# A four-layer graph network on one core: in the search for edges, TensorE's order within a turn and the grouping of three blocks are changed

## The chip, the cores and the metric

The kernel runs on one core of a Trainium2 chip. The metric is the device time of one execution in microseconds (us). Five engines work at once, each through its own instructions in order: TensorE (PE in the profile, its weight loads PEld), VectorE (DVE), ScalarE (ACT), GpSimd (POOL) and SyncE (SP). SP, ACT and POOL also issue DMA transfers; POOL alone issues the indirect ones, in which a list of row numbers chooses the rows.

## The reference, cut to what matters

There are 2708 nodes with 512 features each and one weighted adjacency matrix, which is mostly zero. Each layer is a sum over neighbours, added to its input and normalised along the features.

```
x = layernorm(x + d*(adj+I)*d @ x @ W0.T + b0)          # d: row sums to the power -1/2
x = layernorm(x + (inc @ x) / rowsum(inc))               # inc = adj + (adj>0)/sqrt(count of adj>0)
x = layernorm(x + sigmoid(ga * softmax-like(adj) @ (x@Wsa) + gb * (adj @ x @ Wg + bg)))
x = layernorm(x + relu(adj @ (x>0) @ sign(W3).T))
```

All four layers use the same nonzero pattern of `adj`. A zero entry adds nothing in any of them.

## The kernel before

The nodes are cut into 22 blocks of 128 rows, the last (21) of 20. `adj` is dense in memory and mostly zero, so the kernel first **searches**: for every block of output rows it finds the nodes that have an edge to it, lists them in tiles of 128, and fetches only those rows of the transposed matrix into `packed[b]`. The number of tiles of each block is fixed ahead (`ROOM`: 4, 4, 3 and 1 for blocks 18 to 21). Afterwards the four layers multiply the packed tiles with gathered feature rows.

The search goes in **turns**, `turn(at)`, one for each block in the order 1 to 21 and then 0 (`arrival`). Blocks are handled in **groups** (`GROUPS`): the lists of a group are made together, some turns after its last block. Within a turn all engines' instructions are kept in the order in which the code calls the steps (`in_order`), so the order of the calls is each engine's order. The steps are:

- `load_x`, `load` (SP): the features and the adjacency rows of the block two turns ahead, `arow`, in two halves of 128x1408 and 128x1300. There are four such buffers, so a load waits until the halves of two blocks before have been read.
- `sum_rows` (ACT, L840): row sums of the block's two halves. `degrees` (L848 to L683) makes `dinv` of them for two blocks at a time.
- `mark` (DVE L904, L911, L917; PE L925): a 0/1 mask of the nonzeros, and then 22 small products that count, for each node, the block's edges. They go to a PSUM tile `find`, one for each group out of a ring of two. The remaining steps of VectorE are mixed in between the two halves of the mask.
- `own_diagonals`, `count` (DVE L936 to L981): one turn after the group's last block, the counts become places in a list. `count_partitions` (PE L989) follows after the marks of that turn.
- `steps_of` (DVE L1000 to L1005, PE L1008), `look_up` (ACT L1017, DVE L1029 and L1034, PE L1041) and `keep_looked` (ACT L1051), two turns after it, and `list_nodes` (DVE L1059 to L1078), three turns after it, turn the places into row numbers, `row_at`. For the group (2, 3) all of this happens in the turn after its last block.
- `fetch` (POOL L1099): one indirect DMA of 128 rows for every listed tile. After every second one of the earlier groups a short memset (L1105) makes POOL rest; `RESTED` leaves out the last groups.
- `transpose_x` (PE L1118), `keep_transposed` (ACT L1125), `project0` (PE L1133, four fp32 products of 128x512, shown as eight records), `scale0` (ACT L1142, L1143), `fold` (DVE L1150, L1154) and `grow0` (PE L1161): the first layer's features times `W0`. `y_rows` in memory receives each block's product, and block 0, which is dense, is summed on the way.

Before the change, TensorE's turn `at` is: `steps_of`, marks of block `at`, `count_partitions`, transposes of block `at`, `look_up`, product of block `at-1`, `grow0` of `at-3`.

After the search the layers run over `sequence` = 0, 1, 21, 2, ..., 20. POOL gathers the rows (L626: `xg` from `y_rows` in the first layer, from `x1_rows`, shown as x_rows, in the second), PE multiplies (L1396 in both), DVE and ACT normalise (L1511, L688 to L704). While the first layer runs, the heads of the second are made for one group at a time, at fixed places of `sequence` (`between`): `count_positive` (DVE L1191, PE L1193) and then `head_steps` (DVE L1213 to L1232, ACT L1219, PE L1237, ACT L1245). In the first layer and later, a scheduler mixes the steps of neighbouring blocks. The first gather of a layer waits for all rows that the layer before has written.

Of the kernel before, what the change touches and what calls it, by code (L numbers as in the profile page):

```python
# [52 lines left out]
)  # L53

GROUPS = (
    (1,), (2, 3), (4, 5), (6, 7, 8), (9, 10, 11), (12, 13, 14), (15, 16, 17), (18, 19, 20), (21,),
)


# [448 lines left out]
def sparse_layers(ctx, tc, x, adj, adj_t, w0_t, b0, w_sa, a_sa, w_gcnb, b_gcnb, wa, ba, wb, bb, w3_t,  # L508
# [19 lines left out]
    def rows(b: int) -> int:  # L528
        return min(P, N - b * P)
# [5 lines left out]
    def tiles(b: int) -> int:  # L535
        return len(direct(b)) + ROOM[b]
# [50 lines left out]
    def narrow(b: int) -> int:  # L587
        return len(SPANS[SPLIT[b]])
# [82 lines left out]
    def newton_steps(dst, v, r0, r1, n: int):  # L671
        def square():
            if n == 1:
                nc.vector.scalar_tensor_tensor(r1, r0, v, r0, op0=ALU.mult, op1=ALU.mult)
            else:
                nc.vector.tensor_tensor(r1, r0, v, op=ALU.mult)
                nc.vector.tensor_tensor(r1, r1, r0, op=ALU.mult)

        return [
            lambda: nc.vector.reciprocal(r0, r0),  # L680
            square,
            lambda: nc.vector.tensor_scalar(r1, r1, -0.5, 1.5, op0=ALU.mult, op1=ALU.add),
            lambda: nc.vector.tensor_tensor(dst, r0, r1, op=ALU.mult),  # L683
        ]
# [34 lines left out]
    with tc.tile_pool(name="s_pre", bufs=1) as pre:  # L719
# [65 lines left out]
        turn_at, at = {}, 0  # L785
        for g in GROUPS:
            turn_at[g] = at
            for b in g:
                n, more = narrow(b), ROOM[b] - narrow(b)
# [54 lines left out]
        def degrees(bs):  # L844

            b, n, m = bs[0], len(bs), rows(bs[0])
            deg = small.tile([P, 2], F32, tag="deg", name=f"deg{b}")[:m, :n]
            nc.vector.scalar_tensor_tensor(  # L848
                deg, row_sums[:m, b : b + n, 0], 1.0, row_sums[:m, b : b + n, 1],
                op0=ALU.add, op1=ALU.add,  # L850
            )
            root_ = small.tile([P, 2, 2], F32, tag="root", name=f"root{b}")
            nc.scalar.activation(root_[:m, 0, :n], deg, AF.Sqrt)
            return newton_steps(
                dinv[:m, b : b + n], deg, root_[:m, 0, :n], root_[:m, 1, :n], n
            )

        def due_degrees(at: int):

            if at == NTURN or at == NTURN - 1:  # L860
                return (arrival[at - 1],)
            return tuple(arrival[at - 2 : at]) if 0 < at < NTURN and at % 2 == 0 else ()
# [67 lines left out]
        def own_diagonals(g):  # L930

            b0_, G, m = g[0], len(g), rows(g[0])
            if own_by_itself(b0_):
                own = search[g]["find"][:, b0_ * KINDS : (b0_ + G * (NB + 1)) * KINDS]
                own = own.rearrange("p (g q) -> p g q", g=G)
                nc.vector.scalar_tensor_tensor(  # L936
                    dia_own[:m, b0_ : b0_ + G], own[:m, :, KINDS - 1], 0.0,
                    dia[:m, b0_ : b0_ + G], op0=ALU.is_equal, op1=ALU.mult,
                )

                own = own[:m, :, : KINDS - 1]
                nc.vector.tensor_tensor(own, own, foreign[:m, b0_ : b0_ + G, :], op=ALU.add)
# [43 lines left out]
        def count_partitions(g):  # L986

            b0_, G = g[0], len(g)
            nc.tensor.matmul(  # L989
                search[g]["before"].rearrange("p (c g) -> p c g", g=G), tri,  # L990
                found[:, :, b0_ : b0_ + G], start=True, stop=True,
            )

        def steps_of(g):

            b0_, G = g[0], len(g)
            n = KINDS * G
            diff = search[g]["diff"]
            base = small.tile([P, 2, KINDS * GM], F32, tag="base", name=f"base{b0_}")
            nc.vector.tensor_copy(base[:, 0, :n], search[g]["before"])  # L1000
            nc.vector.tensor_scalar(
                base[:, 1, :n], base[:, 0, :n], WHOLE128, WHOLE128, op0=ALU.add, op1=ALU.subtract
            )
            nc.vector.tensor_copy(table[:, :n, NB], base[:, 1, :n])
            nc.vector.tensor_tensor(  # L1005
                table[:, :n, NB + 1], base[:, 0, :n], base[:, 1, :n], op=ALU.subtract
            )
            nc.tensor.matmul(  # L1008
                diff, step, table[:, :n].rearrange("p k c -> p (k c)"), start=True, stop=True
            )  # L1010
            search[g]["base"] = base
# [36 lines left out]
        def keep_looked(g):  # L1048
            T = sum(ROOM[b] for b in g)
            look = pre.tile([P, TS, NT], F32, tag="look", name=f"look{g[0]}", bufs=2)  # L1050
            nc.scalar.copy(look[:, :T], search[g]["looked"])  # L1051
            search[g]["look"] = look
# [37 lines left out]
                at += ROOM[b]  # L1090

        to_fetch = []
        RESTED = GROUPS[:-2]
        fetched = [0]
        rest = pre.tile([P, 384], F32, name="s_rest")

        def fetch(n: int):
            for b, t, row in to_fetch[:n]:
                nc.gpsimd.indirect_dma_start(  # L1099
                    out=packed[b][:, t + len(direct(b)), :], out_offset=None, in_=adj_t,  # L1100
                    in_offset=bass.IndirectOffsetOnAxis(ap=row, axis=0), element_offset=b * P,
                )
                fetched[0] += 1
                if group_of[b] in RESTED and fetched[0] % 2 == 0:
                    nc.gpsimd.memset(rest, 0.0)  # L1105
            del to_fetch[:n]
# [145 lines left out]
        def count_block0():  # L1252

            for h, ar in enumerate(arows.pop(0)):
                nc.vector.tensor_scalar(
                    ar, ar, 0.0, 0.0, op0=ALU.is_gt, op1=ALU.add, accum_out=counts0[:, h : h + 1]
                )
# [7 lines left out]
        def each(action, at: int):  # L1265
            if 0 <= at < NTURN:
                action(arrival[at])

        def turn(at: int):
            step_of = {at - last_at[g]: g for g in GROUPS[1:]}  # L1270

            def chain(action, since: int):
                if step_of.get(since, SOON) != SOON:
                    action(step_of[since])

            steps = degrees(due_degrees(at)) if due_degrees(at) else []
            chain(steps_of, 2)
            each(sum_rows, at)
            each(keep_transposed, at - 1)
            found_in = step_of.get(1)  # L1280

            if found_in:
                steps.insert(0, lambda: count(found_in))
                steps.insert(0, lambda: own_diagonals(found_in))
            if at < NTURN and arrival[at]:
                mark(arrival[at], steps)
            else:
                for step_ in steps:
                    step_()
            if found_in:  # L1290
                count_partitions(found_in)
                if found_in == SOON:
                    steps_of(SOON)
            each(load_x, at + 2)
            each(load, at + 2)
            each(transpose_x, at)
            chain(look_up, 2)
            chain(list_nodes, 3)
            if found_in == SOON:
                look_up(SOON)  # L1300
                keep_looked(SOON)
            if at == 0:
                for step_ in (
                    count, count_partitions, steps_of, look_up, keep_looked, list_nodes
                ):
                    step_(GROUPS[0])
            each(scale0, at - 2)
            each(project0, at - 1)
            chain(keep_looked, 2)
            each(fold, at - 3)  # L1310
            each(grow0, at - 3)
            if found_in == SOON:
                list_nodes(SOON)
            fetch(len(to_fetch))
            if at == NTURN:
                count_block0()

        with in_order():
            for at in range(NTURN + 4):
                turn(at)  # L1320
# [87 lines left out]
    with tc.tile_pool(name="s_l0", bufs=10, reuse_waits="tile") as lp:  # L1408
# [60 lines left out]
        def several(*actions):  # L1469
            def act():  # L1470
                for a in actions:
                    a()
            return act
# [2 lines left out]
        counts()  # L1476
        roots()
        several(*others)()
        for n, g in enumerate(GROUPS):
            steps_ = head_steps(g)  # L1480
            between.setdefault(2 + 2 * n, []).append(
                several(lambda g=g: count_positive(g, lp), steps_[0])
            )
            between.setdefault(3 + 2 * n, []).append(several(*steps_[1:]))
# [111 lines left out]
    with tc.tile_pool(name="s_l1", bufs=8, reuse_waits="tile") as lp:  # L1596
# [67 lines left out]
        for at, b in enumerate(sequence):  # L1664
            m = rows(b)
            if b:
# [23 lines left out]
                for i0, r0, w, a in narrow_views(b):  # L1690
                    n = a.shape[1]
# [322 lines left out]
    with tc.tile_pool(name="s_l3", bufs=11, reuse_waits="tile") as lp, \  # L2014
# [96 lines left out]
        for at, b in enumerate(order3):  # L2111
# [21 lines left out]
            for i0 in range(0, tiles(b), CH3):  # L2133
                n = min(CH3, tiles(b) - i0)
# [98 lines left out]
```

## Time and profile before

| | |
|---|---|
| median of 3 runs | 954.33 us (953.72 to 957.76) |
| profiled execution, its own time | 988.11 us |
| its span, first to last instruction | 986.3 us |
| granted TensorE clock, mean | 0.944 |
| busy in the span | PE 87%, DVE 66%, POOL 55%, ACT 39% |
| search | to about 197 us, when POOL issues the first gather of the first layer |
| first layer | 197 to 357 us |
| second, third, fourth layer | from 357, about 575 and about 855 us on |

The profiled execution is 33.8 us longer than the median of the runs. Its durations are of that execution; differences between two programs are read as differences of such executions.

In the timeline a row gives start, duration, engine, line, operation, the tile written and the tiles read, the number of records, and in brackets how long the engine had been idle and what ended it. A wait for several things is put down to the one that came last, and where the engine that is named is not concerned, the label is "issue" or a neighbour's.

### The profile page before, as it was taken

Reading aid. Unit: us, or ns where it says so; the run is one execution under the profiler, and the core shown is the slowest. Engines: PE = TensorE matmul, PEld = TensorE weight load, DVE = VectorE, ACT = ScalarE, POOL = GpSimd, SP = SyncE. Lnnn points to the kernel's source line nnn. Section 1 sums busy time; section 2 is a strip of 40 time slices with the busy share of each in tenths; the row PEclk is TensorE's granted clock in tenths of the full one; section 3 lists DMA queues with packets and bytes.
Section 4 is the critical chain, followed back from the end, with each engine's and each line's share of the span. In section 5 each row is a group of like instructions: output and inputs, shape, how many; then the busy total and the mean of one; then the engine's idle time right before and its main releaser. Section 6 shows DMA issues by size and latency. Waiting matters only on the chain.

```text
span 986.3 us, 12778 instructions
## 1 busy us (share of the span) xinstructions
PE 860.5 (87%) x3659; PEld 452.8 (46%) x3659; DVE 647.5 (66%) x2440; ACT 381.3 (39%) x812; POOL 546.1 (55%) x660
## 2 busy tenths in 40 slices
PE   1898978679787989999999989988999999599983
PEld 1454444222122324555555644544556445278762
DVE  5798876827576865565654447665888776557575
ACT  3666555100000114554543424333444332355463
POOL 2587887687877647776652044553454320067661
PEclk9898899979999989999999989999999999799997
DMA  9999986466766646777654267786687540399985
GB/s 290 342 326 338 323 270 180 143 203 201 237 201 218 202 133 193 225 218 237 184 169 131 97 233 252 257 276 233 240 298 255 179 140 33 92 330 348 295 233 172
DMA packets 93556, 220.05 MB, mean 223 GB/s; under 512 B 13660, under 2 KB 28364, under 8 KB 93476
## 3 DMA queue, kind: packets, MB, share of 16 engines
q0 software_dynamic: 43008, 127.61, 42.5%
q1 hardware_dynamic: 38520, 76.78, 22.8%
q10 hardware_dynamic: 11948, 14.76, 4.7%
q8 instruction: 31, 0.51, 0.2%
q14 instruction: 49, 0.40, 0.1%
HBM read 178.21 MB, written 31.71 MB: 213 GB/s over the span
## 4 chain that ended last, share of the span: by engine, by line
PE 65%; DVE 6%; DMA 4%; issue 4%; POOL 2%; ACT 1%; another core or an unknown queue 1%; ACTq 0%; POOLq 0%; DVEq 0%
PE l L1396 16%; PE h L1622 8%; PE e L1847 6%; PE a L1847 6%; PE l L2102 5%; PE pg L1895 4%; PE pc L1895 3%; PE l L2141 3%; DMA xg<-x_rows,i 2%; PE e L1655 2%; PE l L1457 2%; PE a L1656 2%; PE px L1956 2%; PE xt1p L1615 1%
## 5 line engine op out<-in xcount | busy, mean ns | idle before, releaser
L1099 POOL DMA_INDIRECT a<-in_adj_t_dram,row_at x98 | 108.4, 1107 | 59.9 <-issue 21.5
L626 POOL DMA_INDIRECT xg<-x_rows,i x98 | 95.6, 976 | 71.3 <-PE l L1396 38.9
L626 POOL DMA_INDIRECT xg<-y_rows,i x98 | 97.1, 991 | 33.5 <-issue 19.4
L1396 PE MATMUL l<-xg,a 128*32 128x512 f32 (+3 forms) x196 | 88.0, 651 | 14.0 <-DMA xg<-y_rows,i 13.1
L1133 PE MATMUL y<-s_w,xt 128*128 128x512 f32 (+1 forms) x176 | 93.1, 679 | 3.0 <-ACT xt L1125 3.0
L1823 POOL DMA_INDIRECT xg<-x_rows,i x60 | 60.0, 1000 | 62.6 <-ACT ae L1578 17.7
L626 POOL DMA_INDIRECT xg<-xw_rows,i x70 | 70.8, 1011 | 40.4 <-issue 16.2
L1823 POOL DMA_INDIRECT a<-x_rows,i x38 | 37.1, 976 | 90.2 <-DVE mask L1581 36.9
L1622 PE MATMUL h<-s_wsa,xt 128*128 128x256 f32 (+3 forms) x352 | 81.9, 385 | 0.0
L1622 PEld LDWEIGHTS h<-s_wsa,xt 128*128 128x128 f32 (+1 forms) x352 | 63.8, 186 | 24.8 <-ACT xt L1617 8.5
L840 ACT ACTIVATE unused<-arow 128x1408 uint8<-128x1408 f32 (+3 forms) x44 | 58.5, 1329 | 5.9 <-DMA x_rows<-s_zero 1.5
L1133 PEld LDWEIGHTS y<-s_w,xt 128*128 128x128 f32 (+1 forms) x176 | 36.1, 216 | 44.3 <-issue 40.8
L663 ACT ACTIVATE rsqs<-mv 128x1 f32<-128x1 f32 (+2 forms) x56 | 11.3, 202 | 115.0 <-DVE mv L692 69.6
L2102 PE MATMUL l<-ws,pw 128*128 128x512 f32 (+1 forms) x210 | 51.8, 400 | 4.1 <-DVE pw L2026 4.1
L1847 PE MATMUL a<-xg,a 128*32 128x512 f32 (+2 forms) x120 | 51.2, 629 | 4.0 <-DMA xg<-x_rows,i 4.0
L1847 PE MATMUL e<-xg,ae 128*32 128x512 f32 (+2 forms) x120 | 47.9, 601 | 1.0 <-issue 1.0
L2102 PEld LDWEIGHTS l<-ws,pw 128*128 128x128 f32 (+1 forms) x210 | 40.3, 193 | 14.0 <-DVE pw L2026 4.9
L1396 PEld LDWEIGHTS l<-xg,a 128*32 128x32 f32 (+3 forms) x196 | 20.1, 147 | 57.7 <-issue 39.4
L694 POOL TENSOR_TENSOR rs<-mv,s_neg_half 128x1 f32<-128x1 f32 (+1 forms) x22 | 13.0, 592 | 60.4 <-DVE mv L692 51.0
L1895 PE MATMUL pg<-s_wg,pt 128*128 128x256 f32 (+1 forms) x176 | 45.0, 397 | 1.6 <-ACT pt L1883 1.6
L688 DVE BATCH_NORM_STATS2 st<-t 128x6 f32<-128x512 f32 (+1 forms) x66 | 45.2, 686 | 0.3
L904 DVE TENSOR_SCALAR s_mask<-arow 128x1300 bf16<-128x1300 f32 (+5 forms) x42 | 37.6, 900 | 9.4 <-DMA arow<-in_adj_dram 4.9
(310 smaller groups left out, 1961.4 us busy)
## 6 DMA issues: line engine op xcount, KB each, us to landing
arow<-in_adj_dram SPq DMA_DIRECT2D x21, 704.0 KB
arow<-in_adj_dram SPq DMA_DIRECT2D x21, 650.0 KB
x_rows<-f SPq DMA_DIRECT2D x40, 256.0 KB
aw<-in_adj_t_dram SPq DMA_DIRECT2D x21, 320.0 KB
y_rows<-yt ACTq DMA_DIRECT2D x20, 256.0 KB
x_rows<-h SPq DMA_DIRECT2D x19, 257.0 KB
f<-in_x_dram SPq DMA_DIRECT2D x19, 256.0 KB
h_own<-x_rows SPq DMA_DIRECT2D x19, 256.0 KB
```

Of the source, the lines that this page charges most:

```text
L626: nc.gpsimd.indirect_dma_start(out=t, out_offset=None, in_=src[:, :], in_offset=bass.IndirectOffsetOnAxis(ap=index[b][:, i : i + 1], axis=0),)
L688: nc.vector.bn_stats(st[:m], t[:m])
L840: nc.scalar.activation(unused[:m, : ar.shape[1]], ar, AF.Copy, accum_out=row_sums[:m, b, h : h + 1])
L904: nc.vector.tensor_scalar(mask[:m, c0 + skip : c0 + ar.shape[1]], ar[:, skip:], 0.0, None, op0=ALU.not_equal,)
L1099: nc.gpsimd.indirect_dma_start(out=packed[b][:, t + len(direct(b)), :], out_offset=None, in_=adj_t, in_offset=bass.IndirectOffsetOnAxis(ap ...
L1133: nc.tensor.matmul(ps[:m], xt[:, k, :m], w0[:, k, :], start=(k == 0), stop=(k == KC - 1))
L1396: nc.tensor.matmul(ps[r0:r1], weights, moving, start=(i == order[0]), stop=last_of(b, i, order))
L1622: nc.tensor.matmul(ps, xt[:, k, :m], w[:, k, :], start=(k == 0), stop=(k == KC - 1))
L1823: nc.gpsimd.indirect_dma_start(out=g, out_offset=None, in_=x2_rows[:, :], in_offset=bass.IndirectOffsetOnAxis(ap=index[b][:, t : t + 1], a ...
L1847: nc.tensor.matmul(ps[r0:r1], weights, moving, start=(i == order[0]), stop=last_of(b, i, order))
L1895: nc.tensor.matmul(ps, pt[:, k, :m], w[:, k, :], start=(k == 0), stop=(k == KC - 1))
L2102: nc.tensor.matmul(whole[b], p[:r, h, b * P : (b + 1) * P], g[:r, :], start=(j == 0 and h == 0), stop=(j == NB - 1 and h == 1),)
```

## The change

The list of groups gets one more: (18, 19, 20) becomes (18, 19) and (20). The rest setting still leaves out the groups with blocks 18 to 21. In a turn, the transposes of block `at` come first, then `steps_of`, then `keep_transposed` and the product of block `at-1`, and only then the row sums and the marks of block `at`; `look_up` and `grow0` stay where they were. So TensorE's turn becomes: transposes, `steps_of`, product, marks, `count_partitions`, `look_up`, `grow0`. In the first layer the last group, (21), is given its heads second, at place 4 of the sequence, and all groups from (2, 3) on two places later than before: (20), the last, at places 20 and 21.

```
-    (1,), (2, 3), (4, 5), (6, 7, 8), (9, 10, 11), (12, 13, 14), (15, 16, 17), (18, 19, 20), (21,),
+    (1,), (2, 3), (4, 5), (6, 7, 8), (9, 10, 11), (12, 13, 14), (15, 16, 17), (18, 19), (20,), (21,),
...
-        RESTED = GROUPS[:-2]
+        RESTED = GROUPS[:-3]
...
+            each(transpose_x, at)
             steps = degrees(due_degrees(at)) if due_degrees(at) else []
             chain(steps_of, 2)
+            each(keep_transposed, at - 1)
+            each(project0, at - 1)
             each(sum_rows, at)
-            each(keep_transposed, at - 1)
             found_in = step_of.get(1)
...
             each(load_x, at + 2)
             each(load, at + 2)
-            each(transpose_x, at)
             chain(look_up, 2)
...
             each(scale0, at - 2)
-            each(project0, at - 1)
             chain(keep_looked, 2)
...
-        for n, g in enumerate(GROUPS):
+        for n, g in enumerate((GROUPS[0], GROUPS[-1], *GROUPS[1:-1])):
```

More of the change, by code (lines that the diff above doesn't have):

```diff
@@ L55 @@
 GROUPS = (
-    (1,), (2, 3), (4, 5), (6, 7, 8), (9, 10, 11), (12, 13, 14), (15, 16, 17), (18, 19, 20), (21,),
+    (1,), (2, 3), (4, 5), (6, 7, 8), (9, 10, 11), (12, 13, 14), (15, 16, 17), (18, 19), (20,), (21,),
 )
@@ L1092, in sparse_layers @@
         to_fetch = []
-        RESTED = GROUPS[:-2]
+        RESTED = GROUPS[:-3]
         fetched = [0]
@@ L1274, in chain @@
                     action(step_of[since])
+            each(transpose_x, at)
             steps = degrees(due_degrees(at)) if due_degrees(at) else []
             chain(steps_of, 2)
+            each(keep_transposed, at - 1)
+            each(project0, at - 1)
             each(sum_rows, at)
-            each(keep_transposed, at - 1)
             found_in = step_of.get(1)
@@ L1295, in turn @@
             each(load, at + 2)
-            each(transpose_x, at)
             chain(look_up, 2)
@@ L1307, in turn @@
             each(scale0, at - 2)
-            each(project0, at - 1)
             chain(keep_looked, 2)
@@ L1478, in sparse_layers @@
         several(*others)()
-        for n, g in enumerate(GROUPS):
+        for n, g in enumerate((GROUPS[0], GROUPS[-1], *GROUPS[1:-1])):
             steps_ = head_steps(g)
```

## The prediction

> **What bounds the kernel now.** I begin with the page's slices of the span, 24.66 us each, in which the search fills the first eight.
>
> ```profile
> PE   1898978679787989999999989988999999599983
> DVE  5798876827576865565654447665888776557575
> POOL 2587887687877647776652044553454320067661
> DMA  9999986466766646777654267786687540399985
> GB/s 290 342 326 338 323 270 180 143 203 201 237 201 218 202 133 193 225 218 237 184 169 131 97 233 252 257 276 233 240 298 255 179 140 33 92 330 348 295 233 172
> ```
>
> For five slices, to 123 us, the DMA engines are nine tenths busy or more and move 290 to 342 GB/s: adjacency rows and fetched tiles come as fast as they are moved, and no order of TensorE's changes that much. From the sixth slice the rate falls to 270, 180 and 143. What ends the search is therefore in the last 75 us. There the first layer cannot start before POOL has issued all 98 fetches, for its gathers follow on the same queue. POOL's timeline, the rows before and after each gap:
>
> ```profile
> 158.57 1.56 POOL L1099 DMA_INDIRECT a<-in_adj_t_dram,row_at  x1 [3.02 <-DVE s_own L1150]
> ...
> 173.67 0.43 POOL L1105 MEMSET s_rest<- 128x384 f32 x1
> 180.06 1.40 POOL L1099 DMA_INDIRECT a<-in_adj_t_dram,row_at  x1 [5.96 <-DVE s_own L1150]
> ...
> 195.43 1.44 POOL L1099 DMA_INDIRECT a<-in_adj_t_dram,row_at  x1 [0.30 <-issue]
> 197.18 1.01 POOL L626 DMA_INDIRECT xg<-y_rows,i  x1 [0.30 <-issue]
> ```
>
> Read the brackets. The ten fetches of (15-17) begin at 158.57 after 3.02 us of idleness, and end with their rests at 174.10. Then POOL stands for 5.96 us until `row_at` of (18, 19, 20), written on VectorE at 179.62 to 179.79, and issues twelve fetches (11, and 1 of block 21) without a gap, 180.06 to 197.18, 17.1 us. (The named `s_own` is VectorE's next instruction after `row_at`.) The first product of the layer is at 202.44, after 13.10 us in which TensorE had nothing. So the last **lists**, not the last products, set the end of the search.
>
> Next, how the turns hold up the lists. TensorE's timeline:
>
> ```profile
> 110.19 3.60 PE L1133 MATMUL y<-s_w,xt 128*128 128x512 f32 x8
> ...
> 165.28 0.17 PE L925 MATMUL find<-s_sides,s_mask 20*128 20x5 bf16 x1 [2.39 <-DVE turn L972]
> 166.06 5.40 PE L1133 MATMUL y<-s_w,xt 128*128 128x512 f32 x8
> ```
>
> and the waits from 20 to 180 us (total, number, longest):
>
> ```profile
> PE find L925 <- DVE turn L972: 8.7, 3, 3.5
> ...
> ACT look L1051 <- PE y L1133: 8.5, 2, 4.5
> ```
>
> The marks' last product waits for VectorE's mask, and the block's product, queued behind, then takes 5.40 us where 3.60 is the usual. `look_up` and ScalarE's copy of it come after that product.
>
> [...] 5.40 against 3.60 us, a ratio of 1.5, after an idle time of 2.39. [...] the rows of (15-17)'s list wait for a row sum that stands ahead of them, 1.55 us at 157.23, though they don't read it. [...] Here 5.1 us lie between the issue, 197.18 to 198.19, and the first product at 202.44[...].
>
> **The change part by part.**
>
> *One more group.* It adds a count, `steps_of`, `look_up` and list for (20): 22 small VectorE instructions, two small products and two ScalarE copies, by TensorE's and VectorE's rows of 0.15 to 0.6 us about 5 us of VectorE in the last two turns and behind them. SP's and POOL's instructions keep their number and order; the 98 fetches and the transfers are the same. What moves is when lists are ready. (18, 19) is counted in turn 20, looked up in turn 21 and listed in turn 0, each one turn earlier than (18, 19, 20) was. In before the last turn's look-up work (L1029, L1034 on VectorE, L1041 on TensorE) ran from 173.4 to 179.6; turn by turn, at some 7.5 us each, the same work one turn earlier ends near 172. The lists of (18, 19) need the whole chain `steps_of`, copy, `look_up`, copy, list, so I add 3 us and put its `row_at` at 175.
>
> Against that, (15-17) is now listed behind the count of (18, 19) on VectorE, in order. A count of three blocks took 161.01 to 165.15 (its eight instructions 3.40 us), one of a single block 1.99; for two blocks the sum lies midway, 2.7. In before, VectorE idles 0.17 and 1.55 us amid (15-17)'s list at 154.45 to 158.29, which the count fills. So the list is about 2.7-1.7 = **1.0 us later**, and its fetches start at 159.6 and end at 175.1. Then POOL goes on with (18, 19) at once: eight fetches last to about 186, by when (20) and (21), listed where (18, 19, 20) was at 179.8, are there. Twelve fetches of 17.1 us in all end at 192.2, against 197.18: **-5.0 us**. Bounds: -1, if `row_at` of (18, 19) comes only at 179; -9, if (15-17) is not late and earlier idleness also goes. Beyond that another limit comes in: the first gather also needs all `y_rows`, and ScalarE issued the last write at 184.83[...].
>
> *TensorE's order.* Around the loop the same products are done, so the order pays only where a wait goes. In before the mask's late second half leaves TensorE idle (8.7 us) with a ready product behind it; now the product runs in that time. And `look_up` follows the marks, not the product: ScalarE's 8.5 us behind `y` go in part. What this can give to the end is POOL's idleness before its late groups: 1.04 before 135.49 and 3.02 before 158.57, together 4.06. I take two thirds, **-2.7 us**; the rest is again lost to the marks, which come a product (3.6 us) later. Bounds: -6[...], and a loss, priced under rival C. Of the early groups, (2, 3) may come some 2 us later, for its marks follow a product; POOL's 2.62 idle before 88.58 takes that up, and were that cover gone it would cost 2.
>
> ScalarE's `keep_transposed` now comes ahead of `sum_rows`. Row sums and their `dinv` are then later by one copy, 2 us at most; the waits for `deg` in ScalarE's column stand where nothing of POOL's hangs on them, so nothing is put down. A **new wait**: with (18, 19) and (20) separate, `find` of block 21 takes the ring's slot of (18, 19), so its marks wait for ScalarE's copy of the steps (L1017), which stands behind both row sums of 21. Behind these marks TensorE has `count_partitions` of (20), `look_up` of (18, 19), `grow0` and block 0's transposes. The 20-row marks leave time, so 0 to +2; zero in the sum, as slack in the 175 above.
>
> *Heads.* All groups from (2, 3) go two places later, (20) to places 20 and 21 of 22. At the end of the first layer the rows are:
>
> ```profile
> 350.68 0.75 DVE L1511 SCALAR_TENSOR_TENSOR t<-l,s_dinv,f 128x512 f32<-128x512 f32 x1 [0.17 <-PE l L1396]
> 354.06 0.55 DVE L704 TENSOR_SCALAR f<-t,mv,rs 128x512 f32<-128x512 f32 x1
> 357.48 1.18 POOL L626 DMA_INDIRECT xg<-x_rows,i  x1 [14.65 <-DVE inc L1677]
> ```
>
> POOL waits 14.65 us for the last `x1` row. Between `t` and `f` of block 20 VectorE has 13 instructions now and 32 afterwards, since the head steps of (20) and block 19's norm stand there: 19 more. In before the stretch is 3.38 us, mostly waits between short instructions of 0.15 to 0.5 us. For 19 at about 0.2, 3.8, less what falls into these waits, about half: **+2.0 us**. Bounds +0.3 and +4. Heads made two places later elsewhere lie beside a layer in which TensorE is 132.5 of 160 us busy: nothing.
>
> **Sum:** -5.0 - 2.7 + 2.0 = -5.7 us. The profiled execution took 988.11 (span 986.3, 1.8 around it), so 982.4 is its like after the change. It is 33.8 above the median of the runs; I apply the difference unchanged: 954.33 - 5.7 = **948.6**.
>
> **The rivals.**
>
> *B, the gain is hidden.* `row_at` of (18, 19) is late on VectorE, which does extra count and list work there, or the new `find` wait delays `look_up`, so POOL still starts at about 179. That is the change not doing what it says: the bound becomes the look-up chain again. For it: VectorE in 160 to 180 has few gaps. Against: only 2.7 us of extra work. Time: -1 tail, -1 pace, +2 = 954, up to 955.
>
> *C, slower: the marks come too late for VectorE.* `own_diagonals` (L936) reads the marks' counts in the turn after. Now a product of 3.65 us stands before the marks, and VectorE[...] waits at L936 with the next masks behind it. In before such waits are 1.3 us in two places. If half a product is waited in each of five count turns, +9; with the tail gain of -5, +2 of the heads and +1 of dearer products, about +7: **961**. It decides once marks end after VectorE reaches L936, that is, when VectorE's slack of one turn (a turn is some 7.5 us) is below the product. VectorE is mostly five to eight tenths busy in the search's slices, which leaves 2 to 3 us a turn; hence not likely.
>
> *D, a larger gain.* The product now covers every wait for masks: the 8.7 us of TensorE[...] vanish, and DVE's waits for the looked-up lists too. Pace -8, tail -6, heads +2: **942**. Against: the DMA-bound first five slices cannot give it, so it must come from 75 us.
>
> **How the numbers follow.** About 0.5%, 4.8 us, is what a measurement of this kernel can tell from no change: faster is below 949.6, slower above 959.1. Chances: A, the forecast, 0.53 (0.10 of it within the bound); B 0.23; C 0.14; D 0.10. Faster: 0.43 + 0.10 = 0.53; same: 0.10 + 0.23 = 0.33; slower 0.14. Forecast's own range: 944 to 953. The 8-in-10 range goes from 939.5 (D and the bounds of -9 and -6) to 958.0, which takes in B and the milder part of C; outside lie most of C and little of D.
>
> **What would show it.** In POOL's timeline: fetches of (15-17) beginning near 157 to 160, no gap above 1 us before the twelve last ones, first `xg<-y_rows` gather near 189.5 (192.2 less the pace). A gap of 4 us or more there is B. In TensorE's: products near 3.6 and no wait of `find` on `turn`. In VectorE's waits: L936 on marks below 3 us in all; above 8 is C. At the layer's end: `t` to `f` of block 20 about 5.4 us. The prediction is wrong if the first gather is at 196 or later, if the layers past 360 us differ by more than 2 us in length, or if the early fetches, before 123 us, move by more than 3.

## The result, and the profile after

The changed kernel takes 960.58 us in median (22 runs, 954.89 to 964.69), the kernel before in the same comparison 956.74 (22 runs, 953.72 to 966.2). The ratio is 1.0036, 95% interval 1.0022 to 1.005: 3.4 us **slower**, where 5.7 us faster was forecast. It is below the half per cent that counts as a change here, but on the other side of no change, and beyond the range's upper end of 958.0. Runs more than 1.5% above the fastest of their own kernel are left out of every ratio, so a ratio can differ a little from that of the medians.

The profiled execution after took 960.67 (span 958.9). Beside the 988.11 of before this looks like a gain of 27 us, and nothing of the kind is true. The runs below fell on five chips: the kernel before takes 956 to 958 us in median on three of them, 984 on the fourth and 998 on the fifth. By these figures the profile of before would belong to a chip of the slower kind, and its median of 954.33, like the profile of after, to a quick one; the chips of these two profiles are not known. So the page of after can be read for its own waits, but not subtracted from the page of before. Its slices of the span, 23.97 us each:

```profile
PE   1898798588989989999999989988999999689993
DVE  5789898665667846556544447666888776657676
POOL 2588888788888567776532044554454320067662
DMA  9899996676777556776643277787787551299985
GB/s 287 333 333 336 345 321 185 181 215 201 221 228 231 181 166 208 218 240 206 194 153 121 101 246 253 261 276 263 237 287 264 169 157 44 89 291 350 342 253 190
```

The search now ends in the eighth slice. POOL's timeline of after, the rows where the gaps of 3.02 and 5.96 us were:

```profile
153.72 0.44 POOL L1105 MEMSET s_rest<- 128x384 f32 x1
154.32 1.12 POOL L1099 DMA_INDIRECT a<-in_adj_t_dram,row_at  x1 [0.16 <-DVE base L1001]
...
168.33 0.44 POOL L1105 MEMSET s_rest<- 128x384 f32 x1
168.93 0.94 POOL L1099 DMA_INDIRECT a<-in_adj_t_dram,row_at  x1 [0.16 <-DVE base L1000]
...
184.65 0.95 POOL L626 DMA_INDIRECT xg<-y_rows,i  x1 [0.31 <-DMA s_wsa<-in_w_sa_dram]
```

Both gaps are gone, as forecast: 0.16 us ahead of the fetches of (15-17) and of (18, 19). The mechanism at the tail works. The waits of after from 20 to 180 us:

```profile
DVE s_dia_own L936 <- PE find L925: 4.5, 2, 2.3
...
PE find L925 <- DVE s_mask L911: 4.3, 4, 1.7
PE y L1133 <- ACT xt L1125: 3.7, 2, 2.6
ACT look L1051 <- PE find L925: 2.7, 1, 2.7
```

ScalarE's copy of the `look_up` no longer waits for a product `y` (8.5 us before); its waits for the `look_up` products themselves grew from 7.6 us to 11.8. The first line has grown too: VectorE stands at `own_diagonals` for the marks, rival C's wait, twice for over 2 us, where each such wait of before was under 1.

For a comparison of like with like, both kernels were profiled again on one chip (e12 and e13 below). POOL's timeline there, before first:

```profile
86.52 1.40 POOL L1099 DMA_INDIRECT a<-in_adj_t_dram,row_at  x1 [1.96 <-DVE s_own L1150]
...
172.23 1.39 POOL L1099 DMA_INDIRECT a<-in_adj_t_dram,row_at  x1 [2.04 <-DVE s_own L1150]
...
189.02 1.49 POOL L626 DMA_INDIRECT xg<-y_rows,i  x1 [0.31 <-DMA s_wsa<-in_w_sa_dram]
```

```profile
87.62 1.50 POOL L1099 DMA_INDIRECT a<-in_adj_t_dram,row_at  x1 [0.44 <-DVE s_own L1150]
...
184.85 0.95 POOL L626 DMA_INDIRECT xg<-y_rows,i  x1 [0.30 <-DMA s_wsa<-in_w_sa_dram]
```

On this chip the gap ahead of the last twelve fetches of before is **2.04 us, not 5.96**; ahead of (15-17) it has none at all (0.16). The fetches of (6-8), which begin at 86.52 and 87.62, open a stretch in which POOL of the changed kernel never stands for more than 0.4 us again until the first layer. Stage by stage, from these two executions (a stage ends at POOL's first gather of the next):

| stage, us | e12, before | e13, changed |
|---|---|---|
| search, to the first y gather | 189.0 | 184.8 |
| first layer | 150.2 | 153.8 |
| second | 210.4 | 210.4 |
| third | 294.5 | 294.9 |
| fourth | 115.5 | 116.2 |

The search gives 4.2 us, and the first layer takes 3.6 of them back. Of the 4.2, the gap ahead of the last twelve fetches makes 1.9. Another 2.9 come from POOL's own time for the 53 fetches from (6-8) to (15-17) and their rests, 80.8 us against 83.7, with no gap above 0.4 us inside in either. Here the execution of before was 4 us above its kernel's median, that of the changed kernel at its own; the pair does not show the 3 us of the medians.

### The profile page after: what moved, and what is told of

It is laid out like the page before. It is cut to its first block, busy times and chain, and to the rows that moved or that the text cites. A ratio compares the mean times of both kernels' runs of the same rounds, so it can differ in the third digit from the quotient of the medians.

```text
span 958.9 us, 12810 instructions
## 1 busy us (share of the span) xinstructions
PE 855.6 (89%) x3662; PEld 448.5 (47%) x3662; DVE 649.8 (68%) x2476; ACT 382.9 (40%) x816; POOL 549.5 (57%) x660
## 4 chain that ended last, share of the span: by engine, by line
PE 64%; DVE 10%; DMA 10%; POOL 7%; issue 4%; ACT 1%; ACTq 0%; POOLq 0%; DVEq 0%
PE l L1396 14%; PE h L1622 8%; PE a L1847 6%; PE e L1847 6%; PE l L2102 6%; PE l L2141 4%; DMA xg<-y_rows,i 4%; POOL a L1099 4%; PE pg L1895 3%; PE pc L1895 3%; DMA xg<-x_rows,i 2%; PE e L1655 2%; PE a L1656 2%; DMA a<-in_adj_t_dram,row_at 2%; POOL xg L626 2%
## 5 line engine op out<-in xcount | busy, mean ns | idle before, releaser
L626 POOL DMA_INDIRECT xg<-y_rows,i x98 | 101.7, 1038 | 25.3 <-issue 16.4
L1396 PE MATMUL l<-xg,a 128*32 128x512 f32 (+3 forms) x196 | 92.7, 628 | 17.8 <-DMA xg<-y_rows,i 17.6
L1133 PE MATMUL y<-s_w,xt 128*128 128x512 f32 (+1 forms) x176 | 86.8, 639 | 3.8 <-ACT xt L1125 3.7
L1133 PEld LDWEIGHTS y<-s_w,xt 128*128 128x128 f32 (+1 forms) x176 | 33.8, 202 | 48.8 <-issue 36.6
L663 ACT ACTIVATE rsqs<-mv 128x1 f32<-128x1 f32 (+2 forms) x56 | 11.3, 202 | 100.5 <-DVE mv L692 95.8
```

What stands on the lines that cost most here:

```text
L626: nc.gpsimd.indirect_dma_start(out=t, out_offset=None, in_=src[:, :], in_offset=bass.IndirectOffsetOnAxis(ap=index[b][:, i : i + 1], axis=0),)
L1133: nc.tensor.matmul(ps[:m], xt[:, k, :m], w0[:, k, :], start=(k == 0), stop=(k == KC - 1))
L1396: nc.tensor.matmul(ps[r0:r1], weights, moving, start=(i == order[0]), stop=last_of(b, i, order))
```

## The experiments

Times are medians; ratios are to the kernel before on the same chip, with their 95% intervals. The edits are shown in short.

**One part at a time** (before at 984.0 us). First the kernel before again, no edit (e0):

> The kernel before, unchanged, profiled a second time. The changed kernel's profile shows the search ending 12.5 us earlier (first y gather at 184.65 against 197.18), while the runs say 3 us slower. Theory 1 (the first profile of before caught an execution that the runs do not resemble): this time a span of 950 to 958, POOL's gap before the last twelve fetches under 3 us and the first y gather near 183 to 187, so that there was no tail to win. Theory 2 (the tail gain is real and something later gives it back): first y gather again at 195 to 198 and a later stage of before shorter than that of the changed kernel by 12 or more. Ratio to itself 1.000 within 0.2%.

Ratio 1.000 (0.9965 to 1.0034). Theory 1 as worded fell: the gap of 5.98 us and a y gather at 194.46 are there again. The gap is real, on a chip of this speed. What theory 2 left out is told by the next run (e1), the order alone:

```
 GROUPS, RESTED, heads: as before
+ each(transpose_x, at) first; keep_transposed(at - 1), project0(at - 1) ahead of sum_rows and mark
```

> Only the turn's order is changed (transposes and the preceding block's product first, marks behind); the groups and the heads' places stay. If the order is what costs: ratio 1.003 to 1.006, with the lists of the early groups later. If the order pays as forecast (-2.7 us): 0.997. If the groups or the heads cost: 1.000.

Ratio 1.0041 (1.0008 to 1.0073): the order alone doesn't pay, it costs. The search is not where these two profiles differ: first y gather at 194.40 against 194.46. VectorE's timeline of e1, then TensorE's, show what was lost early:

```profile
49.02 0.14 DVE L1169 TENSOR_TENSOR s_row_sum<-s_row_sums 128x2 f32<-128x2 f32 x1
53.11 0.16 DVE L936 SCALAR_TENSOR_TENSOR s_dia_own<-find,s_dia 128x2 f32<-128x2 f32 x1 [3.95 <-PE find L925]
```

```profile
45.63 6.11 PE L1133 MATMUL y<-s_w,xt 128*128 128x512 f32 x8 [0.99 <-ACT xt L1125]
51.58 0.19 PE L925 MATMUL find<-s_sides,s_no_marks 128*128 128x5 bf16 x2
51.64 0.64 PE L925 MATMUL find<-s_sides,s_mask 128*128 128x5 bf16 x20
```

and TensorE's of before, in e0, at the same marks:

```profile
47.45 0.19 PE L925 MATMUL find<-s_sides,s_no_marks 128*128 128x5 bf16 x2
47.50 0.64 PE L925 MATMUL find<-s_sides,s_mask 128*128 128x5 bf16 x20
48.00 0.64 PE L1118 MATMUL pt<-s_ident,f 128*128 128x128 f32 x4
48.68 3.70 PE L1133 MATMUL y<-s_w,xt 128*128 128x512 f32 x8
```

Block 5's marks were ready at 48.1; with the product ahead of them, itself late by a copy and taking 6.11 us where the one in e0 takes 3.70, they end at 52.3, and VectorE, whose next instruction is `own_diagonals` of (4, 5), loses 3.95 us with all that follows. POOL's fetches of (6-8) slip with it:

```profile
88.20 1.50 POOL L1099 DMA_INDIRECT a<-in_adj_t_dram,row_at  x1 [2.14 <-DVE s_own L1150]
```

```profile
91.32 1.50 POOL L1099 DMA_INDIRECT a<-in_adj_t_dram,row_at  x1 [4.53 <-DVE s_own L1150]
```

(e0, then e1.) From there on VectorE waits less, 6.1 us in 125 to 185 us against 11.3, and the gap at the tail shrinks from 5.98 to 3.38. So in the search a delay of 3.1 at the head of an almost unbroken chain and a saving behind it cancel. Where the loss of the ratio lies, the two profiles don't show.

The groups alone (e2), with the old order, the heads of (20) and (21) at one place:

```
+GROUPS: (18, 19), (20,), (21,); RESTED = GROUPS[:-3]
+n = min(n, 8)        # places of the heads
```

> Only the groups are changed: (18,19) and (20), the rests left out as in the changed kernel; the old turn order; the heads of (20) and (21) are both made at places 18 and 19, so nothing falls later than before. If the split pays at the tail as forecast: 0.995. If there is no tail to win (theory 1) and the split's own work costs: 1.000 to 1.003. If order or heads are the cause of the loss: 1.000.

Ratio 1.0011 (0.9987 to 1.0035), y gather at 195.25: nothing won. POOL's gap ahead of the tail is 2.91, but one of 6.67 stands before (15-17). The list of (15-17) now waits behind the count of (18, 19), and there VectorE stands 2.60 us at L936, a wait that the profile ends with a product of `look_up` (L1041), and 3.53 at L1169, ahead of the list, for a row sum: the forecast had put 1.0 us on all that.

The changed kernel with those old heads (e3):

> The changed kernel with its new order and groups, but the heads of (2,3) to (18,19) at the places of before and those of (20) and (21) together at places 18 and 19. If the late heads cost their +2.0 us: ratio 1.0015, that is 0.2% below the changed kernel's 1.0036. If the heads are the whole loss: 1.000 or below. If they cost nothing: 1.0036.

Ratio 1.0009 (0.9984 to 1.0034), y gather at 194.16. The interval holds all but the whole loss; it doesn't settle the heads. But this pair shows the search on the slower chip: the gap at the tail closed from 5.98 us to 0.84, and (6-8) began at 92.97 instead of 88.20, so 0.3 us were left at the first gather.

**The early wait removed** (before at 998.4 us). e4 is the changed kernel, e5 to e7 are it with

```
+ahead = at >= 6      # e5, and e6 with the old heads;  e7: at < 6
+if ahead: new order, else: old order
```

> The changed kernel itself, for a comparison with before and with the next three on one chip. Theory (the tail's gain is eaten early): VectorE waits 2 to 4 us at L936 for the marks at about 52 us, fetches of (6-8) start 3 to 5 us later than in before, POOL is then without a gap to the first y gather, which comes within 1 us of that of before. Ratio 1.002 to 1.005, as measured. If the loss lay in the layers alone, the first y gather would come 3 us or more earlier than in before.

> The changed kernel, but the turns of blocks 1 to 6 keep the old order; the new one begins with block 7's turn. Theory: VectorE's wait at L936 for block 5's marks falls below 1 us, fetches of (6-8) start as in before, near 88, with POOL gapless after it the first y gather comes 3 to 4 us earlier than in the changed kernel; ratio 0.997 to 1.000. Rival (the early wait doesn't matter, because the loads or the lists set the pace): first y gather and ratio as in the changed kernel, 1.0036.

> As the run before, and the heads at the old places ((20) and (21) together at places 18 and 19). If late heads cost 2 us: 0.2% below the run before, so 0.995 to 0.998. If they cost nothing: equal to it.

> The opposite: the new order in the turns of blocks 1 to 6 alone, the old one from block 7 on; groups and heads as in the changed kernel. Theory: the early loss without the later gain: wait at L936 of 2 to 4 us, (6-8) 3 to 5 us late, VectorE's late waits back (10 us or more from 125 to 185), first y gather 2 to 4 us later than in the changed kernel, ratio 1.006 to 1.009. Rival (order without effect): 1.0036.

| run | ratio (95%) | first y gather | waits at L936 over 1 us |
|---|---|---|---|
| e4 changed | 1.0117 (1.0041 to 1.0192) | 201.1 | 4.32, 2.76, 1.21 |
| e5 order late | 0.999 (0.9958 to 1.0022) | 198.8 | 1.27, 3.73 |
| e6 late, old heads | 1.0014 (0.9981 to 1.0046) | 195.6 | 1.31 |
| e7 order early | 0.9996 (0.9958 to 1.0034) | 209.3 | 2.45, 1.74, 4.60 |

The gathers stand in the order that the theory gives: with the early wait removed the search ends 2.3 and 5.5 us sooner than in e4, with the early half alone 8 later. But the executions behind these figures had unlike clocks, 0.941 and 0.942 in e5 and e7, 0.954 and 0.955 in e4 and e6, so the order is not shown by them. Nor do the rest of the expectations follow: e7, expected at 1.006 to 1.009, equals before; (6-8) started near 92 in e5, not 88, with the early wait gone; e6, expected 0.2% below e5, lies 0.2% above it, inside the intervals; and in e4 to e6 POOL stands 4.7 to 5.7 us for the list of (15-17). Single runs of a kernel spread over 17 to 24 us on this chip, where before has no profile, so only the places of the waits are taken from these four.

**Ended after the first layer** (before, whole, at 956.3 us). The first layer's rows go to the output, and layers two to four are left out:

```
-nc.sync.dma_start(x1_rows[...], old[:m, :D])
+nc.sync.dma_start(out[...], old[:m, :D])
 l0_ps.close()
+return
```

> The kernel before, ended after the first layer: layers two to four are left out, and the first layer's rows are the output. It is the yardstick for the next three on the same chip: some 355 to 375 us, with the first y gather where the full kernel has it. The full kernels' times spread by 4 to 6 us on the slower chips, mostly in the layers; here a difference of 1.5 us should be seen.

> The changed kernel, ended after the first layer in the same way. If search and first layer hold the loss of 3.4 us: 2 to 5 us above the cut kernel before. If the tail's gain is just eaten early and the heads cost 1 to 2: +1 to +2. If the loss is in layers two to four alone: 0 or below. As forecast: -5.7.

> The changed kernel with the heads at their old places ((20) and (21) together at 18 and 19), ended after the first layer. If the late heads cost what VectorE's rows show between the last t and f (4.55 against 3.38): 1 to 2 us below the cut changed kernel. If the heads are free: equal within 1 us.

> Only the new turn order, old groups and heads, ended after the first layer. If order alone moves POOL's waits from the tail to the early groups without a net gain: 0 to +1 us against the cut kernel before. If order alone costs what its ratio of 1.0041 says: +3 to +5. If it pays: -2 or below.

Medians of 5 runs each: 343.25, 340.23, 344.01 and 342.73. By means and their spread the changed kernel is 2.9 us faster here (standard error 1.1), the order alone 1.4 (0.9). With old heads it is 0.4 slower (0.8): the late heads cost nothing here, against the forecast. The changed kernel's runs also had a higher granted clock, 0.959 in mean against 0.938 for before, and which of the two follows from the other is not shown. First y gathers: 188.5, 185.7, 184.3, 188.9; of the 4.2 us that the kernel with old heads gains in the search, 1.1 are left in the profiles 155 us later (spans of 340.4 and 341.5), and none in the means.

**All on one chip** (before at 958.0 us): before, changed, changed with old heads, and before with a delay.

```
 for at in range(NTURN + 4): turn(at)
+for _ in range(10): nc.gpsimd.memset(rest, 0.0)      # e15
```

> The kernel before, for its profile on the same chip as the next three. If the layers after the first are alike in both kernels: each of the layers two to four within 2 us of the changed kernel's. On a quick chip (954 to 960 us) the gap before POOL's last twelve fetches is about 2 us, as in the cut kernel, on a slow one (980 and more) about 6.

> The changed kernel on the same chip. If search and first layer gain 2 to 4 us, as in the cut kernels, and nothing is given back: ratio 0.996 to 0.998. If a later layer gives it back: 1.002 to 1.005 again, and that layer is longer by 4 us or more in this profile than in the one of before beside it.

> The changed kernel with the heads at the old places. If the late heads cost the second layer and those after it what they win in the first (cut kernels: 341 against 344): ratio 0.998 to 1.001, 3 us below the changed kernel. If the heads are neutral: equal to the changed kernel within 1 us.

> The kernel before, with ten more short memsets on POOL between the last fetch and the first y gather, which start the first layer 4.5 to 6 us later; nothing else changes. If time at the end of the search passes whole to the end of the kernel: +4.5 to +6 us, ratio 1.005 to 1.006. If a later stage gives back what the search takes or wins: 0 to +2.

Ratios: 0.999 (0.9966 to 1.0013), 1.0034 (1.0012 to 1.0055), 1.0013 (0.9992 to 1.0033), 1.0104 (1.0065 to 1.0143). The loss is there again, and the old heads take about half of it off (1.7 us, standard error 0.9). The delay moved the first y gather by 4.9 us, to 193.95, and cost 9.7 in median (6.2 to 13.7 by the interval): more than passed on, against every expectation. (The two profiled executions are 5.0 apart; e12's was 4 us above its median.) The first layer of e15 was 2.2 us longer than that of e12, with the same code. One place where that shows is its end. VectorE's timeline in e12, e15 and e13, from block 20's `t` to its `f`:

```profile
332.45 0.75 DVE L1511 SCALAR_TENSOR_TENSOR t<-l,s_dinv,f 128x512 f32<-128x512 f32 x1 [1.01 <-PE l L1396]
...
335.83 0.55 DVE L704 TENSOR_SCALAR f<-t,mv,rs 128x512 f32<-128x512 f32 x1
```

```profile
338.44 0.75 DVE L1513 SCALAR_TENSOR_TENSOR t<-l,s_dinv,f 128x512 f32<-128x512 f32 x1 [1.11 <-PE l L1398]
...
342.95 0.55 DVE L704 TENSOR_SCALAR f<-t,mv,rs 128x512 f32<-128x512 f32 x1
```

```profile
330.70 0.75 DVE L1511 SCALAR_TENSOR_TENSOR t<-l,s_dinv,f 128x512 f32<-128x512 f32 x1 [0.84 <-PE l L1396]
...
335.26 0.55 DVE L704 TENSOR_SCALAR f<-t,mv,rs 128x512 f32<-128x512 f32 x1
```

3.38 us in before, 4.51 with the delay, 4.56 changed; 4.51 also in e14, whose heads are at the old places. The stretch got longer without the late heads. The order of the instructions in the traces shows what happened. Between `t` and `f` VectorE runs 11 instructions in e12, 16 in e15, 18 in e14 and 30 in e13; in the last three the end of the preceding block's norm has moved in. The 12 more of e13, against e14, cost 0.05 us. The scheduler that mixes neighbouring blocks in the first layer gives another order when the search is another: ten memsets on POOL alone reorder VectorE's list from its 621st instruction, at 181.7 us in e12, to the last block's norm near 335 us, and TensorE's from the 919th, at 199.9 us, to 333.7. Behind the first layer the lists of before, of the changed kernel, and of e1, e2, e3 and e15 are the same. So no variant here changes the search alone.

**Ended after the third layer** (before, whole, at 955.8 us): the third layer's rows are copied to the output, and the fourth is left out.

```
 l2_ps.close(); w2.close()
+for b in range(NB): nc.sync.dma_start(out[...], place_of_x(b)[...])
+return
```

> The kernel before, ended after the third layer: the fourth is left out, and the third layer's rows are the output. Yardstick for the next run: some 840 to 860 us on a quick chip.

> The changed kernel, ended after the third layer in the same way. In the profiles the layers two and three are the same within 0.5 us. If the loss of 3 us lies in them all the same (by executions that the profiles did not catch): 2 to 4 us above the cut kernel before. If it lies in the fourth layer: 2 us below, as in the kernels cut after the first layer. If the gain there was chance: within 1 us of it.

842.84 and 847.92 us; by means 4.6 us slower (standard error 1.8). So the loss is there by the end of the third layer. e17 shows the early wait once more (3.42 us at L936, (6-8) at 89.71 against 86.33), a y gather only 0.9 us ahead, 186.3 against 187.2, a first layer of 152.2 against 150.4, and a second of 211.5 against 210.3. In seven profiles with at most one of the two edits (order, split) the second layer took 210.2 to 210.5. With both it took 210.3 to 210.4 in three on quick chips (after, e13, e14), 211.5 in e17, and 210.9 to 213.6 in the five on slower ones (e3 to e7), four of them on a chip where before was not profiled. Pairs on one chip show 1.5 us (e0, e3), 1.1 (e16, e17) and nothing (e12, e13). That may be a part of what is missing; its cause is not shown. The third layer alone took 291.2 to 294.8 us in four profiles of before, so one pair of profiles can't show a loss of 3 us there.

## Why the prediction was wrong, by its steps

- **The tail, -5.0: mis-sized for the quick chips, and lost at the head of the chain on the slower one.** The profile showed a gap of 5.96 us, and the forecast applied -5.7 "unchanged" to a median 33.8 us below it. On the chips where before takes 956 to 958 the gap is 0.83 to 2.04 in the three profiles of before (e8, e12, e16), so in that gap at most 2 us were there to win. Pairs on one chip gave 4.2, 2.8 and 0.9 us at the first y gather there, and 0.3 on the slower one (e0, e3), where the gap closed by 5.1 but (6-8) began 4.8 later. The mechanism at the tail (lists ready one turn sooner, no gap) was right. That e13 still gained 4.2 is in part luck: the gap closed by 1.9, the early delay took 1.1, and 2.9 came from POOL's shorter time from (6-8) to (15-17), which is no term of the forecast. That time was shorter throughout on quick chips, 80.8 to 81.3 us in six profiles with both edits and 82.6 to 83.7 in the four of before (e15 counted in); its cause is not shown.
- **The pace, -2.7: in the search a loss instead.** The waits for `y` went as said, but rival C came true in the early turns: L936 waited 2.2 to 4.0 us for block 5's marks in seven of the eleven profiles with the new order there (the one after, e1, e3, e4, e7, e11, e17). The wait went with the length of the product ahead of those marks. In the four others (e9, e10, e13, e14) it took 3.70 us and the wait was 0.74 or 0.75; in the seven it took 5.20 to 6.37. TensorE's product and VectorE's `own_diagonals` in e13, then in e17:

```profile
47.17 3.70 PE L1133 MATMUL y<-s_w,xt 128*128 128x512 f32 x8 [1.06 <-ACT xt L1125]
51.44 0.16 DVE L936 SCALAR_TENSOR_TENSOR s_dia_own<-find,s_dia 128x2 f32<-128x2 f32 x1 [0.75 <-PE find L925]
```

```profile
45.94 6.37 PE L1133 MATMUL y<-s_w,xt 128*128 128x512 f32 x8 [0.99 <-ACT xt L1125]
52.88 0.16 DVE L936 SCALAR_TENSOR_TENSOR s_dia_own<-find,s_dia 128x2 f32<-128x2 f32 x1 [3.42 <-PE find L925]
```

The forecast had products "near 3.6" and priced such waits by turns; this one lies at the head of POOL's chain. "The rest is again lost to the marks" was the right sentence with the wrong sign for the sum. Its own sign of being wrong, early fetches moved by more than 3 us, came with (6-8) in e3 (4.8), e17 (3.4), e1 (3.1) and e9 (3.2, there without the long product), not in e13 (1.1).
- **The count ahead of (15-17)'s list, 1.0.** In e2 its fetches began 6.7 us after POOL was free, 3.9 later than in e0. With the new order as well, (15-17) had no gap above 0.3 us in the one after, e3, e9, e10, e13, e14 and e17, but one of 4.8 in e4 on the slowest chip. The two edits help each other, though not everywhere, which a sum of parts hid.
- **Heads, +2.0.** The stretch grew by 1.2 us, inside the bounds, but for another reason: it also grows with old heads, and 12 more instructions in it cost 0.05. Whole, the old heads are 1.7 us faster (0.9); cut after the first layer, 3.3 slower (1.1). So the sign stays open.
- **The rest of the first layer, "nothing".** This step failed most: the forecast put nothing on the first layer beside the heads at its end. The first layer was 1.8 to 3.6 us longer in each pair on one quick chip (e12 and e13, e16 and e17, and e8 and e9, whose execution was 3 us above its median). In e13, of the 3.6, the gathers' chain made 1.4 (139.0 to 140.4 for 98 gathers), from the last gather to `t` 1.0, from `t` to `f` 1.2.
- **The rest.** In the profiles the gain of the search is all but gone at the end of the first layer: 339.2 and 338.7 there in e12 and e13. The medians of the cut kernels still give 3 us there, and 5 of the other sign two layers later. The order alone shows the same turn: 1.4 us faster when cut, 1.0041 whole. What makes the remaining 3 to 8 us stays open; the lists of instructions there are equal, and the second layer, 1 to 1.5 us longer in two pairs of three, is all that the profiles hold.
- **A reading.** From the issue of the first gather, 197.18, to the first product, 202.44, it is 5.3 us, not 5.1; no term of the sum hangs on it.

No rival told what happened. B foresaw a small gain in the search, but through lists that come too late for the tail and leave a gap of 4 us or more there; that gap went. C's 961 lies nearest to the 960.6 measured, by luck: its waits at L936 were to exceed 8 us and lengthen the search; in the profile after they are 4.5 in all, and the search got shorter in each pair.

## What to carry to other kernels

Before a gap in a profile is turned into a gain, compare the profiled execution with the median of the runs: where they are 3% apart, as here, the gap may belong to another chip or another execution, and need not be in the number that is to be forecast. A saving at the end of a chain is worth what the head of the same chain doesn't lose: look for who waits first, not only longest, and at the one turn where an engine's next instruction hangs on the moved one, as `own_diagonals` did in e1 (3.95 us). Where a scheduler orders the stage behind, moving anything before it can rewrite that stage, as ten memsets did here, so that stage's cost is an unknown; the experiment for it is a pure delay.

## What the runs showed of the hardware

The same program took 956 to 958, 984 and 998 us in median on different chips. Between e12 and e0 the difference sat in the search (189.0, 194.5), the first layer (150, 160) and the fourth (115.5, 121.6), not in the second (210.4, 210.3); the third was shorter on the slower chip (294.5, 291.2).

The length of four products went with the granted clock under them. In the profile of before the one at 110.19 took 3.60 us at 1.00 and the one at 166.06 took 5.40 at 0.68; in that of after the one at 45.99 took 5.20 at 0.71 and the one at 52.96 took 3.60 at 1.00. The forecast set the 5.40 us beside the idleness of 2.39 ahead of it, but an idle time alone doesn't tell: another product of before stood behind one of 2.04 us and took 3.70, at a granted clock of 1.00.

```profile
157.72 3.70 PE L1133 MATMUL y<-s_w,xt 128*128 128x512 f32 x8 [2.04 <-ACT xt L1125]
```

Ahead of the 5.20 us in after, TensorE was busy for 4.25 of the 6 us from 36 to 42, at a granted clock of 1.00, and for 2.85 of the next 3.99, at 0.53. The product's own wait was 1.14 us. In e1 the product of 6.11 us came after 0.99 us of idleness, with waits of 0.32 to 0.78 among the short products before it; in e13 one came after 1.06 and took 3.70. What lowers the clock is not shown. With much the same wait ahead of products of 3.70 and of 6.37 us (e13, e17), the longer figure is the safe one in pricing a product that is moved behind a wait.
